# Cross-attention and FP4 feed-forward block: the circulant attention step moved from shifted copies to a real Fourier basis

## The chip, the cores and the metric

The kernel runs on one core of a Trainium2 chip. The metric is the device time of one execution in microseconds (us); lower is better. Engine names are those of the profile: PE (matrix products), PEld (its weight loads), DVE (vector engine), ACT (activation engine), POOL and SP (here SP issues nearly all transfers, POOL the adding ones).

## The reference, cut to what matters

x and ctx are 64 x 128 x 256 floats; `_layernorm` is the plain one.

```python
q = layernorm(x) @ Wq + bq;  k = v = ctx @ Wq + bq        # 16 channels
corr = real(ifft(fft(q) * conj(fft(k)))).mean(axis=(0, 1))   # 128 lags, over batch and channel
W_topk, I_topk = top_k(corr, 12);  W_topk = softmax(W_topk)
R3 = sum(w * roll(v, -shift) for w, shift in zip(W_topk, I_topk))
x = x + broadcast_over_16_heads(R3) @ Wout + bout
# feed-forward; fp4() quantises blocks of 16 to FP4 and back
u = fp4(layernorm(x))
h = silu(u @ fp4(w_gate).T) * (u @ fp4(w_up).T)
x = x + fp4(h) @ fp4(w_down).T
```

(In the source `K_TOP = int(2 * log(512))`, which is 12, and the FFT runs over the 128 positions.)

## The kernel before, in words

Tokens lie as 16 groups of rows (`q` = 0..15) of four tiles; a tile is 128 tokens x 256. There are 64 tiles, numbered `t`. Four output tables `O[0..3]` of the attention (128 x 257, the last column a row mean) serve all tiles: group `q` uses `O[q % 4]`.

**Opening.** SP loads x transposed (`xt`, 16 loads), then ctx (`ct`, 8 loads `c0`..`c7` of 1 MB), then `Wo`, `Bo`. PE projects x (L921) and ctx (`pk`, L1053); DVE and ACT normalise into `qT` (L863 to L892); 16 products `pg<-qT,kT` (L1076) add up the 128 x 128 matrix whose circulant sums are the correlation. In the gaps DVE quantises the three weight matrices; SP transposes them (L720).

**Bridge**, from the last `pg` to the first feed-forward product. `pg` is copied twice side by side into `Wcor` (L1091). `skew` (L336) runs seven predicated copies that shift row p by p places, bit by bit; a product with ones (L1365) then gives the 128 lags on every partition. Top 12 by MAX8 and MATCH_REPLACE8 (L1387 to L1406), exponentials on ACT (L1399), the weights into `M` (L1410), and `skew` again, so that `M` is the circulant matrix. PE multiplies it with `Wo` (L1441), `Wp` is scaled by 1/sum (L1446, L1448), and `Vn` (the transposed values, L1372 and L1378) times `Wp` plus `Bo` gives `O` (L1454, L1459, copies L1466).

**x stage** (`x_parts`), for a group: mean `neg` (L459), centring, block maxima, scales, rounding on DVE and ACT, then a transposition into `xT`, on PE for the first two pairs of tiles and by an SP transfer (L642) for the rest. `O` is added to X on DVE (L445) for groups 0 to 2 and by an adding transfer on POOL (L481) from group 3 on.

**Feed-forward** (`group_ops`), for a tile: 18 products `gu` (L1166), SiLU on ACT (L1172), `h` and its block maxima on DVE (L1179, L1189, L1203), scaling on POOL (L1218; three tiles on DVE), rounding on ACT (L1246, L1262), two products with the scales on DVE (`hl`, L1271), a transposition by SP into one of eight homes `hT` (two lie in `Wdn`, two in `kT`; L1306), then 17 products `pd` with Wd (L1315, L1317; below "Wd products"), the sum into X (L1334) and the store (L1341). `gu` has two PSUM slots, which before the first tile serve the bridge as `hot` and `pa`: tile 0 takes over `hot`, tile 1 `pa`, and tile t needs that `h` of tile t-2 is done. `hl` has two buffers of two tiles.

**What sets the order.** Every operation is recorded with a cost and a due time (`op`, class `Order`); a planner picks, engine by engine, the one due first among those it expects to be ready, and the program is emitted in that order. Each engine then runs its queue in order. The due time of a tile's Wd products is

```python
dl=at(t) + SLOT * (LC + GROW * min(t, END) / 64.0 + nt - 1 - i + (LATE if t >= END else 0)),
```

with `SLOT` = 5425 ns, `LC` = 4.5 and `GROW` = 6, so they trail the tile's `gu` by some slots more towards the end. The x stage of group `q` is due `min(MARGIN, LEAD[0] + LEAD[1] * q)` slots ahead of its first tile.

Of the kernel before, what the change touches and what calls it, by code (L numbers as in the profile page):

```python
# [33 lines left out]
SUB = 2.0**-16  # L34
MAGIC_SUB = 1.5 * 2.0**32
# [224 lines left out]
def xattn_ffn(ctx: ExitStack, tc: tile.TileContext, x, xt, cx, wq, bq, wo, bo, wgu, wd, out):  # L260
# [13 lines left out]
    MT = res.tile([P, P], F32, name="MT")  # L274

# [25 lines left out]
    bits_i = const.tile([P, 7], I32, name="bits_i")  # L301
    bits = const.tile([P, 7], U16, name="bits")
# [7 lines left out]
    for k in range(7):  # L310
        V.tensor_single_scalar(bits_i[:, k : k + 1], pidx, 64 >> k, ALU.bitwise_and)
    V.tensor_copy(bits, bits_i)
# [15 lines left out]

    def skew(W, key, **kw):
        for k in range(7):  # L330
            s = 64 >> k
            n = P + s - 1
            op(
                "V",
                220,
                lambda k=k, s=s, n=n: V.copy_predicated(  # L336
                    W[:, 0:n], bits[:, k : k + 1].broadcast_to([P, n]), W[:, s : s + n]
                ),
                w=[key],
                **kw,  # L340
            )

# [4 lines left out]
    LC = 4.5  # L347
# [4 lines left out]
    TC = 46000.0  # L352
    TQ = 42000.0
# [13 lines left out]
    LEAD = (0.5, 0.5)  # L367
# [5 lines left out]
    LOADS = "wq bq wg0 wg1 x0 wg2 x1 x2 x3 wd x4 x5 x6 x7 x8 x9 x10 x11 x12 x13 x14 x15 c0 c1 c2 c3 c4 c5 c6 c7 wo bo"  # L373
# [50 lines left out]
    def x_parts(R, q, i0, nt, fast, due, alu, pe_x=False, root=False, both=None, off=0):  # L424
# [197 lines left out]
        if pe_x:  # L622
            for i in tiles:
                pt = Q["pd"].new()

                def f_t(i=i, pt=pt):
                    for b in range(4):
                        src = T["xhl"].t[:, i, b // 2, (b % 2) * P : (b % 2) * P + P]
                        PE.transpose(pt.t.bitcast(F16)[:, b * P : (b + 1) * P], src, ident_h)

                op("PE", 300, f_t, r=[(T["xhl"], 0), (T["xhl"], 1)], w=[pt])

                def f_x(i=i, pt=pt):
                    dst, src = T["xT"].t[:, i].rearrange("p k n -> p (k n)"), pt.t.bitcast(F16)[:, 0 : 4 * P]
                    V.tensor_copy(dst, src) if fast else A.copy(dst, src)

                op("V" if fast else "A", 420 if fast else 590, f_x, r=[pt], w=[(T["xT"], i)], dl=due - 300, port=False)
        else:
            op(
                "SP",  # L640
                450 * nt,
                lambda: SP.dma_start_transpose(  # L642
                    sub("xT").rearrange("p t k n -> p (t k) n"), sub("xhl").rearrange("p t e n -> p (t e n)")
                ),
                r=[(T["xhl"], 0), (T["xhl"], 1)],
                w=[(T["xT"], i) for i in tiles],
                lat=LT,
                dl=due - 2000,
            )
# [9 lines left out]
    Bo = res.tile([P, D + 1], F32, name="Bo")  # L659
    kT = res.tile([P, 16, P], F32, name="kT")  # L660
    W = res.tile([P, 2 * P], F32, name="Wcor")
# [66 lines left out]
    def d_scales(pool, ring, loaded):  # L728
        dgd = pool.tile([P, P], F32, name="dgd")
# [6 lines left out]
        op("V", 130, lambda: V.tensor_scalar(dgd, ident, s1, None, ALU.mult), r=["s1"], w=["dgd"])  # L736
        pm_d = ring.new()
        op("PE", 430, lambda: PE.matmul(pm_d.t[:, 0:P], ones, dgd, start=True, stop=True), r=["dgd"], w=[pm_d], dl=18000.0)
# [31 lines left out]
    with ExitStack() as ph1:  # L770
# [21 lines left out]
        r_ct = S.ring(rp, "ct", [P, 2, 4, 256], F32, 5)  # L792
# [11 lines left out]
            "bo": (400, ["Bo"], lambda: SP.dma_start(Bo[:, 0:D], bo.partition_broadcast(P))),  # L804
# [10 lines left out]
        for j in range(8):  # L815
            loads[f"c{j}"] = (2580, [(cts[j], 0), (cts[j], 1)], lambda j=j: SP.dma_start(cts[j].t, cx[j]))
            for b in range(2):
                loads[f"c{j}{'ab'[b]}"] = (
                    1456,
                    [(cts[j], b)],  # L820
                    lambda j=j, b=b: SP.dma_start(cts[j].t[:, :, :, b * P : (b + 1) * P], cx[j][:, :, :, b * P : (b + 1) * P]),
                )
# [32 lines left out]
        mrow = wp.tile([P, P], F32, name="mrow")  # L855
# [184 lines left out]
        op("SP", 2464, tr(WgH, lambda: HgN.rearrange("p h c n -> p (h c n)")), r=["HN", (cts[7], 0)], w=["WgH"], dl=TD - 2000, lat=LL, after=prev)  # L1040
        wgl = op("SP", 2464, tr(WgL, lambda: LgN.rearrange("p h c n -> p (h c n)")), r=["LN", (cts[7], 0)], w=["WgL"], dl=TD - 2000, lat=LL, after=prev)
        loaded = (load_x(0, dl=TD, after=(wgl,)),)
        d_scales(wp, r_q, loaded)
        load_x(1, dl=TD + 9000, after=loaded)
        for j, b0, b1 in [(j, 0, 2) for j in range(7)] + [(7, 0, 1), (7, 1, 2)]:
# [4 lines left out]
            def f_k(ct=ct, pk=pk, c0=b0 * P, n=n):  # L1050
                for kt in range(2):
                    for g in range(4):
                        PE.matmul(  # L1053
                            pk.t[32 * g : 32 * g + 32, 0:n],
                            Wq[:, kt],
                            ct.t[:, kt, g, c0 : c0 + n],
                            start=(kt == 0),
                            stop=(kt == 1),
                            tile_position=(0, 32 * g),
                            skip_group_check=True,  # L1060
                        )
# [12 lines left out]
            def f_g(bs=range(2 * j + b0, 2 * j + b1)):  # L1074
# [13 lines left out]
        op(  # L1088
            "V",
            331,  # L1090
            lambda: V.tensor_copy(  # L1091
                W.rearrange("p (a s) -> p a s", a=2), pg.unsqueeze(1).broadcast_to([P, 2, P])
            ),
            r=["pg"],
            w=["W"],
        )
# [258 lines left out]
    M = cs.tile([P, 2 * P], F32, name="M")  # L1355
    Wp = cs.tile([P, 2, D + 1], F32, name="Wp")
    skew(W, "W")
# [7 lines left out]
    sums = op("PE", 220, lambda: PE.matmul(hot.t[:, 512 : 512 + P], ones, W[:, 0:P], start=True, stop=True), r=["W"], w=[pc])  # L1365
    for j in range(8):
        after = () if j < 2 else (sums,)
        pv = Q["pd"].new()

        def f_v(j=j, pv=pv):  # L1370
            for b in range(2):
                PE.transpose(pv.t[:, b * P : (b + 1) * P], kT[:, 2 * j + b], ident)  # L1372

        op("PE", 220, f_v, r=[("kT", 2 * j), ("kT", 2 * j + 1)], w=[pv], after=after)
        op(
            "A",
            270,
            lambda j=j, pv=pv: A.copy(  # L1378
                Vn[:, :, 2 * j : 2 * j + 2, :].rearrange("p g b c -> p b g c"),
                pv.t[:, 0:256].rearrange("p (b g c) -> p b g c", b=2, c=32)[:, :, :, 0:16],  # L1380
            ),
            r=[pv],
            w=["Vn"],
        )

    C = lambda: hot.t[:, 512 : 512 + P]
# [16 lines left out]
    op("A", 1300, lambda: A.activation(warm, c_half, AF.Sqrt), w=["tbl"], dl=TO)  # L1403
# [5 lines left out]
        335,  # L1409
        lambda: V.scalar_tensor_tensor(  # L1410
            M.rearrange("p (a s) -> p a s", a=2),
            C3.unsqueeze(1).broadcast_to([P, 2, P]),
            NEG,
            E.unsqueeze(1).broadcast_to([P, 2, P]),
# [5 lines left out]
        w=["M", "es"],  # L1420
    )
    skew(M, "M")
    op("V", 69, lambda: V.tensor_scalar(es, es, 0.5, None, ALU.mult), w=["es"])
    op("V", 75, lambda: V.reciprocal(es, es), w=["es"])

    jw = cs.tile([P, D], BF16, name="jw")
    for dst, key in ((Wo[:, 0], "Wo"), (Wo[:, 1], "Wo"), (Bo, "Bo")):
        op(
            "A",
            400,  # L1430
            lambda dst=dst: A.activation(
                jw, dst[:, 0:D], AF.Copy, scale=1.0 / D, accum_out=dst[:, D : D + 1]
            ),
            w=[key, "jw"],
        )
    for k in range(2):
        pr = Q["pd"].new()
        op(
            "PE",
            430,  # L1440
            lambda k=k, pr=pr: PE.matmul(pr.t[:, 0 : D + 1], M[:, 0:P], Wo[:, k], start=True, stop=True),  # L1441
            r=["M", "Wo"],
            w=[pr],
        )
        if k == 0:
            f = lambda pr=pr: A.activation(Wp[:, 0], pr.t[:, 0 : D + 1], AF.Copy, scale=es)  # L1446
        else:
            f = lambda pr=pr: V.tensor_scalar(Wp[:, 1], pr.t[:, 0 : D + 1], es, None, ALU.mult)  # L1448
        op("AV"[k], 390, f, r=[pr, "es"], w=[("Wp", k)])
    pb = Q["pd"].new()  # L1450
    for g in range(4):
        po, pn = ((pa, g), pa.t[:, 512 * g : 512 * g + D + 1]) if g < 3 else ((pb, 0), pb.t[:, 0 : D + 1])
        Vg = Vn[:, g].rearrange("p b (r e) -> p e (b r)", e=2)
        op("PE", 430, lambda pn=pn: PE.matmul(pn, ones[0:1], Bo[0:1], start=True, stop=False), r=["Bo"], w=[po], after=(sums,))  # L1454
        for e in range(2):
            op(
                "PE",
                430,
                lambda e=e, pn=pn, Vg=Vg: PE.matmul(pn, Vg[:, e], Wp[:, e], start=False, stop=(e == 1)),  # L1459
                r=["Vn", ("Wp", e)],  # L1460
# [5 lines left out]
            lambda g=g, pn=pn: A.copy(O[g], pn),  # L1466
            r=[po],
# [4 lines left out]
    for t in h_tiles:  # L1472
        op(
            "A",
            350,
            lambda t=t: A.activation(
                t[:, :, NF : NF + 2 * NB], ones[:, 0 : 2 * NB].unsqueeze(1).broadcast_to([P, 2, 2 * NB]), AF.Copy, scale=htiny
# [107 lines left out]
```

## Time and profile before

| | us |
|---|---|
| three runs | 439.36, 439.63, 443.25; median 439.63 |
| the profiled execution, own time | 438.03 |
| its span, first to last instruction | 435.9 |
| busy PE / DVE / ACT / POOL | 415.9 / 388.7 / 286.2 / 136.9 |
| mean granted clock of PE | 0.999 |
| last `pg` product to first `gu` product | 54.7 to 73.57 |
| first to last `gu` product (starts) | 73.57 to 409.0 |

Times below are microseconds from the start of the span. A line of the timeline gives start, duration, engine, line of the kernel, operation, output and inputs, shape and count; a bracket holds the idle time of the engine before it and who ended it. Matmuls overlap, so their start-to-start distance (0.43 us for two `gu` products of 512 columns) tells more than their duration. A line of waits gives the total, the count and the longest.

### The profile page before, as it was taken

To read this page: it belongs to the slowest core of one execution; us is meant where nothing else is said; L and a number is where in the kernel's file an instruction comes from. 1 tells how busy PE (TensorE), PEld (TensorE's weight loads), DVE (VectorE), ACT (ScalarE), POOL (GpSimd) and SP (SyncE) were. 2 spreads that over 40 slices of the span, in tenths; PEclk is the share of its full clock that TensorE was granted. 3 is DMA by queue.
4 is the path that set the end of the run, shared out by engine and by line. 5 is a ranking of instruction groups with operands and counts; after the bars stand their busy time and mean duration, and the time that the engine had idled before them with its cause. 6 is when DMAs were issued, how large, how long until landed. Compare 5 with 4: busy or idle time off the path is not lost.

```text
span 435.9 us, 7976 instructions
## 1 busy us (share of the span) xinstructions
PE 415.9 (95%) x2948; PEld 265.4 (61%) x2948; DVE 388.7 (89%) x832; ACT 286.2 (66%) x484; POOL 136.9 (31%) x121
## 2 busy tenths in 40 slices
PE   7999978889899999999999999999999999999996
PEld 6457655446555656566566666666665666566685
DVE  6999368999999999989999989999999999978872
ACT  2797547988596696467946794887579666464410
POOL 0000003044444264344444444454434222324100
PEclk9999999999999999999999999999999999999999
DMA  7999999253787588579767897687578615952362
GB/s 282 408 415 420 334 215 358 37 105 71 151 185 142 131 196 175 139 117 233 157 136 161 197 158 163 139 176 152 117 161 164 156 39 120 192 125 66 94 169 74
DMA packets 151495, 76.61 MB, mean 176 GB/s; under 512 B 134432, under 2 KB 141984, under 8 KB 150432
## 3 DMA queue, kind: packets, MB, share of 16 engines
q1 hardware_dynamic: 143968, 69.29, 59.5%
q0 software_dynamic: 7488, 6.82, 11.0%
q8 instruction: 23, 0.38, 0.4%
q14 instruction: 16, 0.13, 0.1%
HBM read 27.76 MB, written 8.39 MB: 83 GB/s over the span
## 4 chain that ended last, share of the span: by engine, by line
PE 61%; DVE 16%; DMA 9%; ACT 9%; issue 2%; SPq 1%; DVEq 0%; ACTq 0%
PE gu L1166 37%; PE pd L1315 14%; PE pd L1317 8%; DMA ct<-in_cx_dram 6%; DMA xt<-in_xt_dram 4%; DVE hs L1189 3%; DVE h L1179 2%; DVE hl L1271 2%; ACT junk L507 2%; ACT cc L497 2%; ACT g L1172 2%; DVE am L517 1%; ACT hk L1246 1%; ACT hc L1262 1%; DVE hr L1203 1%
## 5 line engine op out<-in xcount | busy, mean ns | idle before, releaser
L1166 PE MATMUL gu<-WgH,xT 128*128 128x512 f16 (+1 forms) x768 | 191.7, 361 | 5.5 <-ACT g L1172 1.5
L1166 PEld LDWEIGHTS <-xT 128*128 128x128 f16 x1152 | 112.4, 98 | 114.8 <-issue 4.5
L1218 POOL TENSOR_TENSOR h<-h,hr 128x704 f32<-128x704 f32 x61 | 92.8, 1521 | 199.0 <-DVE hr L1203 169.7
L1166 PE MATMUL gu<-WgL,xT 128*128 128x512 f16 (+1 forms) x384 | 107.4, 361 | 0.0
L1172 ACT ACTIVATE g<-gu,ug 128x704 f32<-128x704 f32 x64 | 53.6, 840 | 41.8 <-PE gu L1166 41.6
L1246 ACT ACTIVATE hk<-h,c_half 128x1408 int16<-128x1408 f32 (+1 forms) x34 | 47.4, 1394 | 37.3 <-POOL h L1218 34.5
L1189 DVE TENSOR_REDUCE hs<-h 128x44 f32<-128x792 f32 x64 | 66.7, 1042 | 2.1
L481 POOL DMA_DIRECT2D X<-O x52 | 45.7, 939 | 71.0 <-DMA X<-in_x_dram 71.0
L1179 DVE SCALAR_TENSOR_TENSOR h<-gu,uh,g 128x704 f32<-128x704 f32 x64 | 55.9, 874 | 5.0 <-ACT g L1172 3.2
L1262 ACT ACTIVATE hc<-hk,c_sub 128x1408 f16<-128x1408 int16 (+1 forms) x32 | 45.6, 1426 | 0.5
L1315 PE MATMUL pd<-WdH,hT 128*128 128x256 f16 x352 | 43.7, 273 | 1.2 <-DMA hT<-hl 1.2
L1315 PEld LDWEIGHTS <-hT 128*128 128x128 f16 x352 | 34.3, 98 | 9.5 <-DMA hT<-hl 1.6
L1334 DVE SCALAR_TENSOR_TENSOR X<-pd,ud,X 128x512 f32<-128x512 f32 (+1 forms) x34 | 24.3, 715 | 11.3 <-PE pd L1317 11.3
L497 ACT ACTIVATE cc<-X,neg 128x256 f32<-128x256 f32 x62 | 30.2, 497 | 3.6 <-DVE neg L459 2.9
L1271 DVE TENSOR_TENSOR hl<-hc,hsb 128x1408 f16<-128x1408 f16 (+1 forms) x34 | 28.7, 843 | 0.2
L1271 DVE TENSOR_TENSOR hl<-hc,hsl 128x1408 f16<-128x1408 f16 (+1 forms) x34 | 28.6, 841 | 0.0
L1203 DVE RECIPROCAL hr<-hs 128x44 f32<-128x44 f32 x64 | 26.8, 419 | 0.2
L507 ACT ACTIVATE junk<-cc 128x256 bf16<-128x256 f32 x64 | 25.9, 405 | 1.0 <-DVE cc L470 0.8
L1317 PE MATMUL pd<-WdL,hT 128*128 128x256 f16 x192 | 26.2, 273 | 0.0
L1232 ACT ACTIVATE hsb<-hs 128x176 bf16<-128x176 f32 (+1 forms) x34 | 11.4, 334 | 19.8 <-DVE hs L1189 19.8
L912 ACT ACTIVATE xsq<-xt,shift 128x1024 f32<-128x1024 f32 x16 | 18.1, 1148 | 9.5 <-DVE shift L908 7.0
L584 DVE TENSOR_TENSOR cc<-cc,rz 128x256 f32<-128x256 f32 x64 | 23.3, 418 | 0.1
(215 smaller groups left out, 532.9 us busy)
## 6 DMA issues: line engine op xcount, KB each, us to landing
xt<-in_xt_dram SPq DMA_DIRECT2D x16, 512.0 KB, 8.1
ct<-in_cx_dram SPq DMA_DIRECT2D x8, 1024.0 KB, 11.5
X<-in_x_dram SPq DMA_DIRECT2D x16, 512.0 KB, 4.5
out_dram<-X SPq DMA_DIRECT2D x30, 256.0 KB, 2.3
X<-O POOLq DMA_DIRECT2D x52, 128.0 KB, 2.8
Wg<-in_wgu_dram SPq DMA_DIRECT2D x2, 512.0 KB, 4.5
Wdn<-in_wd_dram SPq DMA_DIRECT2D x1, 704.0 KB, 9.6
hT<-hl SPq DMA_TRANSPOSE x32, 3.3
```

Source lines behind the costliest of these rows:

```text
L481: lambda i=i: G.dma_start(Xq.t[:, i0 + i], O[g][:, 0:D], accum_op=ALU.add),
L497: lambda i=i: A.activation(T["cc"].t[:, i], Xq.t[:, i0 + i], AF.Identity, bias=T["neg"].t[:, i : i + 1]),
L1166: PE.matmul(pg.t[:, c0:c1], src[:, b], w[:, k, c0:c1], start=(m == 0), stop=(m == 5))
L1172: lambda pg=pg, g=g: A.activation(g.t, pg.t[:, 0:NF], AF.Silu, scale=ug),
L1179: lambda pg=pg, g=g, i=i: V.scalar_tensor_tensor(B["h"].t[:, i, 0:NF], pg.t[:, NF:NG], uh, g.t, ALU.mult, ALU.mult),
L1189: lambda i=i: V.tensor_reduce(B["s"].t[:, i], B["h"].t[:, i].rearrange("p (jj b e) -> p b jj e", b=NB, e=2), AX.XY, ALU.max, apply_absolut ...
L1218: lambda i=i, zv=zv: (V if zv else G).tensor_tensor(per_block(B["h"].t[:, i, 0:NF], NB), per_block(B["h"].t[:, i, 0:NF], NB), spread(B["r" ...
L1246: lambda: A.activation(sub("k"), sub("h")[:, :, 0:NF], AF.Identity, bias=c_half, scale=24.0),
L1262: lambda: A.activation(flat("c"), flat("k"), AF.Identity, bias=c_sub, scale=SUB),
L1271: lambda e=e, part=part: V.tensor_tensor(B["hl"].t[:, 0:nt, e].rearrange("p t (jj n) -> p t jj n", jj=JJ), sub("c").rearrange("p t (jj n) ...
L1315: PE.matmul(pd, hT.t[:, b], WdH[:, :, b], start=(b == 0), stop=False)
L1317: PE.matmul(pd, hT.t[:, b], WdL[:, :, b], start=False, stop=(b == 5))
```

## The change

1. `skew` and its 14 predicated copies are gone. DVE makes a 128 x 128 table of sines and cosines during the opening (a saw-tooth of the index, folded, then a polynomial; `four`), PE transposes it (`fourT`).
2. Correlation: `pg` is copied once, one product with `fourT`, two products-with-sum on DVE give `uv`, two products bring the 128 lags onto every partition.
3. The weights `wm` are summed against the table (`wv`). Products of `Wo` and of `Vn` with the table (`J`, `B`, `Va`) do not need them and are issued ahead; `Wp` is put together from `J`, `B` and `wv`, and 1/sum is applied in the copies to `O`. The row means of `Wo` and `Bo` move from ACT to DVE.
4. ctx is laid out in half blocks, `c7` loaded as two; `Bo` is loaded into one partition, ahead of `c0`.
5. `LC` is 5.5 and `LEAD` (1.5, 0.5); the first `xT` copies are due 4 us earlier; the small constants in the `h` tiles (`least`) go from ACT to POOL.

```diff
-    LC = 4.5
+    LC = 5.5
-    LEAD = (0.5, 0.5)
+    LEAD = (1.5, 0.5)
-    LOADS = "... x15 c0 c1 c2 c3 c4 c5 c6 c7 wo bo"
+    LOADS = "... x15 bo c0 c1 c2 c3 c4 c5 c6 c7a c7b wo"
...
+        op("G", 300, lambda: G.iota(ang(), pattern=[[0, 2], [1, P]], base=0, channel_multiplier=0), w=[(scr, "ang")])
+        for k in range(2):
+            op("V", 170, lambda k=k: V.tensor_scalar(ang()[:, k], ang()[:, k], fr, 96.0 * k, ALU.mult, ALU.add), ...)
+        op("V", 300, lambda: V.tensor_single_scalar(ang(), ang(), 127, ALU.bitwise_and), w=[(scr, "ang")])
...
+        op("V", 330, lambda: V.scalar_tensor_tensor(four[:, 0:2], poly(), SIN[0], tri(), ALU.add, ALU.mult), ...)
...
-            W.rearrange("p (a s) -> p a s", a=2), pg.unsqueeze(1).broadcast_to([P, 2, P])
+        op("V", 220, lambda: V.tensor_copy(W, pg), r=["pg"], w=["W", "mrow"], dl=TC + 4000.0)
-    skew(W, "W")
-    sums = op("PE", 220, lambda: PE.matmul(hot.t[:, 512 : 512 + P], ones, W[:, 0:P], ...), r=["W"], w=[pc])
+    T_op = op("PE", 270, lambda: PE.matmul(C(), fourT[:, 0], W, start=True, stop=True), r=["W", "fourT"], w=[pc])
+    for k in range(2):
+            lambda k=k: V.scalar_tensor_tensor(jk, C(), wt, four[:, 2 + k], ALU.mult, ALU.mult, accum_out=uv[:, k : k + 1]),
+            PE.matmul(C(), uv[:, k : k + 1].broadcast_to([P, P]), four[:, k], start=(k == 0), stop=(k == 1))
...
-    skew(M, "M")
+    for k in (1, 0):
+            lambda k=k: V.scalar_tensor_tensor(jk, wm, (wt, nwt)[k], four[:, k], ALU.mult, ALU.mult, accum_out=wv[:, k : k + 1]),
+    op("V", 75, lambda: V.reciprocal(inv, es), r=["es"], w=["inv"])
+    op("V", 200, lambda: V.tensor_scalar(Wp[:, 0], JB, wv[:, 1:2], None, ALU.mult), ...)
+    t1_op = op("A", 450, lambda: A.activation(Wp[:, 1], spec["J", 1][1](), AF.Copy, scale=wv[:, 1:2]), ...)
+    op("A", 1300, lambda: A.activation(warm, c_half, AF.Sqrt), w=["tbl"], dl=TO, after=[*quick, t1_op])
+            lambda e=e, t=t: V.scalar_tensor_tensor(Wp[:, e], t(), wv[:, 0:1], Wp[:, e], ALU.mult, ALU.add),
+    for g in range(4):
+        bank = (2, 0, 1, 2)[g]
+            lambda pn=pn: PE.matmul(pn, es[0:1, 0:1].broadcast_to([1, P]), Bo, start=True, stop=False),
+                lambda e=e, pn=pn, Vg=Vg: PE.matmul(pn, Vg[:, e], Wp[:, e], start=False, stop=(e == 1)),
+            lambda g=g, pn=pn: A.activation(O[g], pn, AF.Copy, scale=inv),
```

As emitted, the tables `O[2]` and `O[3]` are finished after the first tile's `gu` products, on ACT behind a load of its function table, and in the same PSUM slot that tile 1's `gu` takes over.

## The prediction

> **What bounds the kernel now.** I read the chain that ended last first, then the engines by stretches, then the timeline of the bridge, then the waits of PE behind it.
>
> ```profile
> PE 61%; DVE 16%; DMA 9%; ACT 9%; issue 2%; SPq 1%; DVEq 0%; ACTq 0%
> ```
>
> ```profile
> 55.00:73.50 18.50, 14.77 (x86) 11.06 (x86) 14.15 (x52) 10.32 (x34) 1.01 (x2) 1.00 1.07 290
> 73.50:90.00 16.50, 13.98 (x76) 7.27 (x77) 16.33 (x39) 15.65 (x36) 3.54 (x4) 1.00 0.41 87
> 90.00:110.00 20.00, 20.00 (x117) 11.28 (x116) 19.60 (x47) 16.48 (x36) 10.52 (x9) 1.00 0.43 86
> 110.00:140.00 30.00, 26.32 (x166) 15.65 (x164) 29.48 (x67) 21.31 (x40) 12.77 (x12) 1.00 0.78 168
> 140.00:409.00 269.00, 267.69 (x1698) 165.90 (x1696) 252.51 (x492) 180.88 (x286) 108.17 (x89) 1.00 0.69 148
> ```
>
> Columns: stretch, length, busy time of PE, PEld, DVE, ACT, POOL, granted clock, DMA share, GB/s. From 140 to 409 PE is full and only its own work counts. From 73.5 to 140 DVE is full and PE stands still for 2.5 and 3.7 us. Before that neither is full: a chain through all engines sets the pace.
>
> ```profile
> 53.12 1.60 PE L1076 MATMUL pg<-qT,kT 128*128 128x128 f32 x12
> 54.77 0.42 DVE L1091 COPY Wcor<-pg 128x256 f32<-128x256 f32 x1 [7.38 <-PE pg L1076]
> 55.23 2.49 DVE L336 COPY_PREDICATED Wcor<-bits,Wcor 128x191 f32<-128x191 uint16 x7
> 61.34 1.70 DVE L336 COPY_PREDICATED M<-bits,M 128x143 f32<-128x143 uint16 x5
> 63.15 1.11 PE L1441 MATMUL pd<-Wo,M 128*128 128x257 f32 x4 [0.80 <-issue]
> 66.42 0.23 DVE L459 TENSOR_SCALAR neg<-MT,O 128x2 f32<-128x2 f32 x1 [1.64 <-ACT O L1466]
> 73.57 0.60 PE L1166 MATMUL gu<-WgH,xT 128*128 128x512 f16 x2 [0.56 <-DVE xT L635]
> 77.19 1.28 ACT L1495 ACT_TABLE_LOAD   x1
> ```
>
> The bridge takes 11.65 us from the copy at 54.77 to `neg` at 66.42, some 5 of them in two skews; another 7.15 lead to the first product at 73.57.
>
> ```profile
> PE gu L1166 <- DVE h L1179: 1.3, 1, 1.3
> PE pd L1315 <- DMA hT<-hl: 1.2, 1, 1.2
> PE pd L1315 <- DMA Wdn<-hl: 1.1, 1, 1.1
> PE gu L1166 <- ACT xT L635: 1.0, 1, 1.0
> PE gu L1166 <- DMA xT<-xhl: 0.8, 1, 0.8
> ```
>
> These are PE's waits between 66 and 141: twice for transposed `hl` (Wd products issued before their input), three times for h or xT.
>
> **Part 1, up to the last pg.** DVE gains the table. Six operations with two inputs of 128x256 at 0.35 start to start (L584: two in 0.76), four with one input at 0.25 (L592 takes 0.33 at twice the width), six of half width at 0.15 to 0.25 and a small reduction: 2.1 + 1.0 + 1.1 + 0.45, about 4.7 us; bounds 4 and 6. The cover is the 7.38 us that DVE idles ahead of L1091. As emitted, ten of these stand ahead of the chain rstd, qT, but the third LgN (0.94), a Wdn product (0.88) and the small scales (1.2) move behind it, so that chain stays within 0.3 us. PE's order changes: all four fan products (L873) now run first, ending near 45.3 (before 45.66), and after them come four `pk` (0.97 each), two halves (1.24), 16 `pg` (0.27 each) and three transpositions (0.47): 9.9, so the last `pg` ends at 55.2 instead of 54.72. That is +0.5; bounds -0.3 (PE fills its waits as before) and +4.7 (the whole table ahead of qT).
>
> The halved c7 buys nothing here: PE reaches its first half at 51.8, and the whole block landed at 51.3. The layout reads 4 KB runs instead of 8 KB. xt, which has 4 KB runs, moved 406 to 411 GB/s, ct 416 to 426, so 8.4 MB of ct take up to 0.6 us more; PE comes to the second half at 52.9, 1.0 later than even that. The Trainium skill (DMA: Bandwidth & Descriptors, Bandwidth) advises transfers of at least 1 MiB for 75% of peak, which speaks against halves; xt's 512 KB loads at 408 GB/s do not bear it out. By that page's table (0.95 us for 64 KB, 6.15 for 1 MB) I estimate two halves at 0.6 us more than one whole: by it the second half would land at 52.5, and the sum would stay. The 1 KB of Bo ahead of c0 costs one issue (0.58 at L804) in SP's queue, whose eight ct issues are spread over 16.3 us anyway, waiting for buffers.
>
> **Part 2, the bridge.** Out go the skews (2.49 and, 60.55 to 63.04, another 2.49) and the Wo product with its copy on the path. In its place, from 55.2: copy 0.30 (L863 reads PSUM at this width in 0.29); table product to its reader 0.64 (57.72 to 58.36 for L1365); two sums at 0.35 (L1410: 0.42 at twice the width plus a 0.08 read); two products to MAX8 0.96; MAX8 to the last weighting 1.73, unchanged (58.36 to 60.09); weighting 0.37; `wv`, 1/sum, `wv` 0.86; `Wp` 0.35 and two additions at 0.45 (L1448: 0.48); the last product 0.70; 0.30 because it stands behind its partner in PE's queue; the copy to `O` 0.41. Sum 8.2 (the accumulating forms and the broadcast weights are not in the trace: bounds 7.2, all at the rows of half the width, and 9.8, all at the full width). So `neg` runs at 63.45, 2.97 earlier. The sums of Wo (L517 at this width: 0.69) hide in the 0.96; the products J, B and Va hide on PE behind the MAX8 part; without that cover they cost eight times 0.55.
>
> The Sqrt table load (1.28, next operation 1.29 after it starts) now stands on ACT right ahead of O[0]; it ends at 62.6 and O's product at 62.95, so it is covered by 0.35. The Trainium skill (ScalarE: Activation LUTs, What ACT_TABLE_LOAD costs) adds a 1.38 us drain to each switch; the trace shows none here, but by that rule `neg` would come 1.0 later. X0 landed at 61.3 and X1 at 68.0, against needs at 63.7 and 69.5: the loads hide, X1 by 1.5 us only.
>
> The 7.15 us of the x stage are the same instructions, so the first `gu` starts at 70.6, -3.0.
>
> **Part 3, where the lead goes.** Tile 1's slot holds O[2] and O[3]. ACT copies them only behind the Silu table load, which ended 12.3 us after `neg`: 75.7, then some 0.5 later for the X addition moved back, then two copies. Tile 1 starts at 77.2, as before. It costs little: tile 2 (81.95) needs xT, and tile 3 needs h of tile 1, which DVE finishes at 85.7. I walked the emitted order with start-to-start times of the same rows: h of tile 0 at 80.75, then hs 1.0, a rounding 0.4, two xhl 1.35. Tile 3 starts at 85.8 against 88.75.
>
> Then the due times act. The first Wd product follows 7.3 tiles of `gu` instead of 5.7, and the lag stays 0.7 to 1 tile longer. Tile 4 starts at 90.6 (92.3 before), tile 6 at 98.4. `xhl` of group 2 ends on DVE at 109.05; its transfers make tile 8 start at 113.2 against 116.44, with PE idle for 4.0, and with two Wd products (3.7) fewer done. They are made up without waits: tile 12 starts at 134.9 against 136.5, six Wd products done in both. **Lead 1.6 to 1.7 us.** From here PE is full. Before lost another 1.3 after this point (0.97 at 174 for a SiLU); I take half of that as saved. Sum: -1.7 - 0.65 = -2.35.
>
> POOL's three small constants wait for O[3] at 77.1 and take 0.4 to 1.5 each (L1218 has four times the size), so they end between 78.3 and 81.6; the first hs runs at 81.6. Behind them in POOL's queue stand four adding transfers for group 3 (0.9 to 2.2 each, 2.8 to land), which land by 93 at the latest; ACT takes that group up after 95. SP's queue keeps its order of weights and X; an xT transfer waits behind one hT transfer, which is in the 113.2.
>
> The profiled execution, 438.03, becomes 435.7; the median of the runs shown stands 1.6 above it, so 439.63 becomes **437.3**.
>
> **Rivals.**
> *The early lead stays and the waits go* (faster): 2.95 at tile 3 plus the Wd, xT and h waits behind it (1.2, 1.1, 0.8, 0.6, 0.97) give -7.5, 432.1. For it: these are waits for inputs a tile late, which a longer lag meets. Against it: DVE is busy 29.5 of 30 us there, and its work is not less.
> *The lead is lost* before tile 12 (pg 1 us later, X1 or the table load late): 439.6.
> *The homes of hT* (slower): eight homes, and the lag of Wd products reaches 13.0 tiles instead of 12.0. Tile 58's transposition ran at 405.52, its home was free at 399.4, tile 59's at 402.2. As emitted those two Wd products move 1.33 tiles of `gu` (4.8 us) later, which eats the margin. If from the point where the lag exceeds what `gu` to `hl` takes plus eight, half of the last 17 pairs wait one Wd product (1.86), DVE, which idles under 1% from 200 to 350, pays 14.9, less 4.7 of slack at the end (hl of tile 63 at 422.9, transposed at 427.65), less 2.35: +7.8, 447.5. For it: SP already waits nine times on pd. Against it: never over 1.3 us.
>
> **How the numbers follow.** Forecast 0.50, lead lost 0.13, faster rival 0.25, slower rival 0.12. The forecast's own range is -4.2 (parts 1 and 2 at their lower ends: 0.8 and 1.0 off) to +0.5 (PE loses after tile 8 the 3.0 that it lost there before: 113.2 + 3.7 - 116.4): 435.4 to 440.1. The upper end of part 1 alone, with all of the table ahead of qT, gives +1.9, 441.5. The 8 in 10 takes that in and reaches towards both rivals: 432.0 to 442.5. One per cent, 4.4 us, is about what a measurement of this kernel can tell from no change: faster 0.25, same 0.62, slower 0.13.
>
> **What would show it.** The MAX8 at 57.75 and `neg` near 63.45; the first `gu` near 70.6, the second tile near 77.2; PE idle some 4 us ahead of tile 8; tile 12 near 134.9; the last `gu` near 407. Wrong if pg ends after 56, if ACT's load is what O[0] waits for, or if SP's waits on pd grow past 2 us.

## The result, and the profile after

The changed kernel takes 441.25 us (median of 20 runs, 439.28 to 444.02), the kernel before 439.37 (20 runs, 437.8 to 443.25): ratio 1.0044, interval 1.0025 to 1.0063. It is 1.9 us slower where 2.35 us faster was forecast.

The chain that ended last, of the changed kernel, and its engines by the stretches of before (columns as there; the granted clock is the third number from the end):

```profile
PE 73%; DVE 10%; ACT 8%; DMA 6%; issue 2%; SPq 1%; POOL 0%; ACTq 0%; DVEq 0%; POOLq 0%
```

```profile
55.00:73.50 18.50, 15.32 (x64) 9.63 (x63) 11.91 (x45) 10.85 (x32) 0.22 (x1) 0.85 1.07 278
73.50:90.00 16.50, 14.95 (x74) 8.15 (x73) 13.82 (x33) 12.81 (x31) 6.74 (x8) 0.86 0.37 78
90.00:110.00 20.00, 19.60 (x110) 10.57 (x109) 19.79 (x49) 15.67 (x29) 9.34 (x8) 1.00 0.51 89
110.00:140.00 30.00, 25.51 (x154) 15.36 (x153) 27.83 (x61) 24.07 (x49) 11.68 (x10) 0.89 0.72 142
140.00:409.00 269.00, 266.87 (x1685) 164.58 (x1683) 252.23 (x495) 179.88 (x283) 109.59 (x90) 1.00 0.79 149
```

The new thing is the clock: 1.00 in all these rows before, now 0.85, 0.86 and 0.89 in three. Finer windows show that it is 1.00 or 0.50 and changes on a grid of 3.41 us, which lies elsewhere in each execution:

```profile
64.43:67.85 3.42, 2.40 (x9) 1.51 (x10) 2.52 (x6) 1.78 (x8) 0.00 (x0) 1.00 0.89 238
67.85:71.26 3.41, 2.84 (x8) 1.47 (x7) 3.02 (x13) 2.75 (x11) 0.00 (x0) 0.50 1.02 404
71.26:74.67 3.41, 3.41 (x17) 2.44 (x17) 1.82 (x6) 2.28 (x9) 1.39 (x2) 0.50 1.02 417
74.67:78.09 3.42, 3.42 (x10) 1.22 (x9) 3.35 (x10) 2.59 (x9) 2.00 (x3) 0.50 0.36 79
112.22:115.63 3.41, 1.33 (x8) 0.56 (x6) 3.38 (x8) 1.38 (x4) 1.01 (x1) 1.00 0.86 165
115.63:119.05 3.42, 1.02 (x3) 0.43 (x4) 3.39 (x8) 2.85 (x2) 2.97 (x4) 0.50 1.09 194
119.05:122.46 3.41, 3.41 (x10) 1.21 (x8) 3.41 (x16) 1.73 (x6) 0.69 (x1) 0.50 0.70 127
```

Five stretches at half clock, behind two places where PE had too little to do: the bridge, and the pause ahead of tile 8. This profiled execution is the longest of the 20. An execution's stretches follow from its mean clock: (1 - clock) x span / 0.5 / 3.41, rounded. Median spans by their number, with how many executions in brackets:

| kernel | 0 | 1 | 2 | 3 | 4 and more |
|---|---|---|---|---|---|
| before (27, beside e1 to e4) | 435.9 (7) | | 437.4 (18) | 439.1 (1) | 440.9 (1) |
| changed | | 437.6 (2) | 439.3 (13) | 440.5 (2) | 441.5, 442.2 (3) |
| e1_fill | | 438.0 (5) | 439.2 (7) | | |
| e5_fill_both | 436.8 (5) | 437.3 (5) | 440.0 (2) | | |
| e6_fill_t8 | 436.1 (4) | 437.8 (8) | | | |
| e9_fill_grow5 | 435.5 (7) | 436.7 (5) | | | |
| e10_t8_grow5 | 435.0 (3) | 435.9 (1) | 437.8, 438.1 (2) | 438.7 (5) | 440.4 (1) |
| e12_onerow | | 437.1 (4) | 438.4 (8) | | |
| e13_bias_rows | | 437.7 (7) | 438.8 (4) | | 440.2 (1) |
| e14_best | 434.9 (10) | 434.6 (1) | 436.5 (1) | | |

The bridge and the pause, by the timeline of the changed kernel (start, length, engine, line; in brackets the idle time before and what ended it):

```profile
56.99 0.30 DVE L1464 MAX8 ma<-gu 128x8 f32<-128x128 f32 x1
61.41 0.49 DVE L1515 SCALAR_TENSOR_TENSOR Wp<-gu,wv,Wp 128x257 f32<-128x257 f32 x1 [0.91 <-ACT Wp L1508]
64.50 0.23 DVE L454 TENSOR_SCALAR neg<-MT,O 128x2 f32<-128x2 f32 x1 [2.22 <-ACT O L1541]
66.42 0.37 ACT L1461 COPY Va<-gu 128x256 f32<-128x256 f32 x1 [0.79 <-PE gu L1526]
66.69 0.42 ACT L502 ACTIVATE junk<-cc 128x256 bf16<-128x256 f32 x1
75.08 1.06 PE L1190 MATMUL gu<-WgH,xT 128*128 128x512 f16 x2
118.03 1.04 PE L1190 MATMUL gu<-WgH,xT 128*128 128x512 f16 x2 [4.49 <-DVE h L1203]
```

MAX8 and `neg` come earlier than before (58.36, 66.42), the first `gu` later (73.57): its two matmuls take 1.06 where 0.60 is usual. PE stands still for 4.49 ahead of tile 8. The bracket names the `h` that ended at 118.01; the transfer of tile 8's `xT` had landed only 0.02 earlier, at 117.99, and in e1 below the same pause ends with that transfer.

### The profile page after: what moved, and what is told of

The parts are those of the page before. It is cut to its first block, busy times and chain, and to the rows that moved or that the text cites. A ratio compares the mean times of both kernels' runs of the same rounds, so it can differ in the third digit from the quotient of the medians.

```text
span 442.2 us, 7970 instructions
## 1 busy us (share of the span) xinstructions
PE 422.5 (96%) x2934; PEld 268.2 (61%) x2934; DVE 390.9 (88%) x847; ACT 286.6 (65%) x477; POOL 140.1 (32%) x125
## 4 chain that ended last, share of the span: by engine, by line
PE 73%; DVE 10%; ACT 8%; DMA 6%; issue 2%; SPq 1%; POOL 0%; ACTq 0%; DVEq 0%; POOLq 0%
PE gu L1190 42%; PE pd L1339 15%; PE pd L1341 8%; DMA xt<-in_xt_dram 4%; DVE hs L1213 2%; DVE h L1203 2%; ACT g L1196 1%; DMA Wg<-in_wgu_dram 1%; DVE hl L1295 1%; PE pk L1047 1%; PE gu L1534 1%; PE pg L1070 1%; PE pm L867 1%; ACT hk L1270 1%; ACT hc L1286 1%
## 5 line engine op out<-in xcount | busy, mean ns | idle before, releaser
L1190 PE MATMUL gu<-WgH,xT 128*128 128x512 f16 (+1 forms) x768 | 194.8, 365 | 8.6 <-DVE h L1203 4.8
L1190 PE MATMUL gu<-WgL,xT 128*128 128x512 f16 (+1 forms) x384 | 108.8, 365 | 0.0
L593 ACT ACTIVATE k<-cc,c_half 128x1024 int16<-128x1024 f32 (+1 forms) x16 | 17.9, 1118 | 8.6 <-DVE cc L579 8.6
```

What stands on the lines that cost most here:

```text
L1190: PE.matmul(pg.t[:, c0:c1], src[:, b], w[:, k, c0:c1], start=(m == 0), stop=(m == 5))
```

## Experiments

**Fill in the bridge, with and without.** The kernel has identity products (L719, L724 before) that its emitter puts into PE's idle time as planned. In the bridge the kernel before has 16 of them, the changed one 4, since the planner books each new product at 530 ns and sees no idle time. e1_fill brings them to 16 (12 more, not the six that its expectation names); e2_nofill takes all but one of them out of the kernel before.

```
- for _ in range(int((at - self.free["PE"] - SPARE) / cost)):
+ for _ in range(o.extra + max(0, int((at - self.free["PE"] - SPARE) / cost))):
...  # e1: extra = 2 at the Va product of g 2, and at bias and Wp·Va for g > 0
     heat_buf(hot, TW)
+    S.fill.pop()   # e2, in the kernel before
```

> Theory A (clock): between the last pg and the first gu the changed kernel issues 4 fill products (identity by identity, L719) where the kernel before had 16, because its planner counts the new products at 530 ns each and sees no idle time; PE then streams for too small a share of one 3.41 us stretch and the granted clock falls to 0.5 for one or more whole stretches, each of which costs 1.7 us. Six fill products more, in the places where PE waits for ACT's copies, should hold the clock through the bridge: mean clock 0.996 or more in most executions, the time 1.5 to 3 us below the changed kernel's 441.25, at 438 to 439.7, ratio to before 0.997 to 1.001. Theory B (order): the clock only follows from PE's waits, and the time is lost to the order on ACT and PE (O[0] behind Va copies, tile 1 behind O[2] and O[3]); then the fill gains nothing and the ratio stays at 1.003 to 1.006.

> The kernel before without the 16 fill products of the bridge (they write nothing that is read). Theory A: PE streams for under half of at least one stretch of 3.41 us, the clock falls to 0.5 for 2 to 4 stretches, mean clock 0.985 to 0.992, and the time rises by 2 to 5 us, ratio 1.005 to 1.011. Theory B: the bridge is set by ACT and DVE, fill is idle work, ratio 0.999 to 1.001.

e1: 440.68, 1.0033 (1.0018 to 1.0047). e2: 441.17, 1.0049 (1.0031 to 1.0068), with three stretches or more in every execution. In the kernel before the fill is not idle work: without it the time rises. e1's ratio lies in Theory B's range, not in Theory A's: its trace shows the bridge at full clock, as Theory A said, but it gained only 0.6, with the stretches behind tile 8's pause still there:

```profile
65.30:68.71 3.41, 3.27 (x18) 2.55 (x17) 2.33 (x8) 2.36 (x10) 0.00 (x0) 1.00 0.89 347
109.54:112.96 3.42, 0.12 (x1) 0.00 (x0) 3.38 (x9) 1.53 (x2) 2.23 (x2) 1.00 1.10 209
112.96:116.37 3.41, 2.30 (x6) 0.89 (x7) 3.38 (x13) 3.19 (x5) 2.44 (x3) 0.50 1.09 203
116.37:119.78 3.41, 3.41 (x11) 1.36 (x9) 3.34 (x11) 1.08 (x4) 0.00 (x0) 0.50 0.39 65
```

**The due times.** e3_old_due sets LC 4.5 and LEAD (0.5, 0.5) in the changed kernel, e4_new_due the new values in the kernel before, e7_fill_lc LC 4.5 in e1_fill.

> The changed kernel with the due times of before (LC 4.5, LEAD 0.5), so only the Fourier part is left and the early xT copies. Theory A: the stretch at 112 to 116 us, where PE stood still ahead of tile 8, keeps more Wd products and the clock stays full there; only the bridge's stretches at half clock are left: mean clock 0.992 to 0.996 and 438.5 to 440, ratio 0.998 to 1.002. Theory B: the later due times saved waits, as forecast; without them 1 us more than the changed kernel, ratio 1.005 to 1.008.

> The kernel before with the later due times alone (LC 5.5, LEAD 1.5). Forecast's reading: fewer waits for hT, 0.5 to 1 us saved, ratio 0.997 to 0.999. Theory A: Wd products that filled PE's waits between 100 and 120 us are put off, PE stands still longer there, and one or two stretches at half clock appear ahead of tile 8: mean clock 0.992 to 0.996, ratio 1.003 to 1.008. If due times do not matter at all: 0.999 to 1.001.

> The fill of e1_fill, and the Wd products' due time back at LC 4.5 (LEAD stays at 1.5). Theory A: real work takes the place of the pause: four Wd products instead of two are done when tile 8 starts, as before, so the stretches there stay full as before: mean clock 0.996 or more; but a Wd product waits for hT once or twice (1.2 us each before): 437.5 to 439.5, ratio 0.997 to 1.001. Theory B (the later due times are what the gain hangs on, as e3_old_due's 1.0147 suggests): slower than e1_fill by 1 to 5 us, ratio 1.006 to 1.015.

e3: 445.57, 1.0147 (1.0123 to 1.017). e4: 441.39, 1.003 (1.0005 to 1.0054). e7: 444.26, 1.0119 (1.0094 to 1.0144). Theory A missed on e3 and e7; e3 is slower than either theory said, e7 within Theory B. In e7, with four Wd products done, PE waits 7.4 us ahead of tile 8, as DVE makes `xhl` for it at 116.36 instead of 107.75 (e1): earlier Wd work goes ahead of it on the engine that is full. The later due times are needed by the Fourier part. In the kernel before (e4, as Theory A said) they put off work that covered a wait: 2.8 us ahead of tile 8, with a stretch at half clock behind it; its trace has two more, in the bridge and behind the first `gu` products.

**Fill ahead of tile 8**, into its own buffer, overwritten by its products: e5 in e1_fill, e6 in the changed kernel.

```
+ for _ in range(6 if t == 8 and c0 == 0 else 0):
+     PE.matmul(pg.t[:, 0:P], ident, ident, start=True, stop=True)
```

> The fill of e1_fill in the bridge, and 6 identity products (12 instructions, 2.6 us) ahead of the products of tile 8, written into its own buffer and then overwritten; they can start once h of tile 6 is read, some 1.7 us after PE falls idle. Theory A (clock): e1_fill kept the clock full in the bridge and still lost 3.4 us to the two stretches at 112.96, behind the pause of 4.4 us ahead of tile 8. With the pause half filled, these stretches stay full: mean clock 0.998 or more in most executions, span 435.5 to 436.5, time 437.3 to 438.3, ratio 0.996 to 0.999. Theory B (order): the pause is there because xT is late, the time after it is set by DVE, and fill gains under 0.5 us: ratio 1.002 to 1.004 as in e1_fill.

> The changed kernel with the 6 identity products ahead of tile 8 alone, no fill added in the bridge. Theory A: the stretches behind tile 8's pause go (3.4 us, two stretches), those of the bridge stay (1 to 3 stretches, 0.75 to 1.7 us each): mean clock 0.989 to 0.997, 438 to 440, ratio 0.998 to 1.002. Theory B: as the changed kernel, 1.004.

e5: 438.98, 1.0006 (0.9978 to 1.0034). e6: 439.32, 0.9999 (0.9975 to 1.0024). e6 is within Theory A; e5 lies between the two theories, as only 5 of its 12 executions have no stretch at half clock. Some 2 us come back with work that computes nothing: the slowdown against the kernel before goes with the clock. In executions with no stretch at half clock e5 and e6 stand at 436.8 and 436.1, the kernel before, run beside them, at 435.8: the forecast gain is not there at full clock either.

**ACT's queue in the bridge.** e8_va_dve is e5 with three Va copies (L1461) on DVE.

> As e5_fill_both, and the copies of Va for the groups 1 to 3 are on DVE instead of ACT. In e1_fill ACT read the squares for the first x tile 2.18 us after neg, where the kernel before took 0.78: two Va copies stood ahead of them in ACT's queue, each waiting for PE. If that is where the bridge's lead of some 2 us at neg shrank to 0.9 us at the first gu, the first gu comes 0.8 to 1.4 us earlier than in e5_fill_both (near 71.5 instead of 72.7), and tile 1 near 77.5; at the end 0 to 1 us of it is left: ratio 0.994 to 0.998. If ACT's queue does not matter there: as e5_fill_both within 0.3 us.

e8: 440.7, 1.005 (1.0029 to 1.0071). The first `gu` came at 71.83 (e5 73.18), as expected; tile 1 at 79.40 and tile 8 at 116.21 (e5 79.14, 114.63). The time missed its range (0.994 to 0.998). A lead at the first `gu` does not reach tile 8: DVE, with no wait between 98 and 118, makes `xhl` for it at 110.50, where e5 has 108.25.

**The lag at the end.** e9 is e5 with 11 products ahead of tile 8 and GROW 5.0 for 6.0, e10 the same without the bridge's fill; e11 is the kernel before.

> As e5_fill_both, with 11 identity products (2.4 us) ahead of tile 8 instead of 6, which took only 1.65 us of the pause, and with GROW 5.0 instead of 6.0: the due times of Wd products then reach 12 tiles of lag at the end, as before, instead of 13. If the clock is what is left ahead of tile 8, the two stretches seen there in e5_fill_both go, and nearly every execution has 0 or 1 stretch at half clock. If the lag is what made PE wait twice for a SiLU near 345 and 366 us (0.87 and 0.86 us; the kernel before has one such wait, 0.97 at 174), one or both go: span 435.2 to 436.3, time 437.0 to 438.2, ratio 0.995 to 0.999. If neither matters: as e5_fill_both, 1.000.

> As e9_fill_grow5 without the fill added in the bridge: the bridge's stretch at half clock stays in two executions of three (0.7 to 1.7 us). Clock theory: 0 to 1.5 us above e9_fill_grow5, ratio 0.996 to 1.001. If the six fill products in the bridge delay the chain more than the clock costs: 0.3 to 0.7 us below e9_fill_grow5.

> The kernel before, unchanged: where its own stretches at half clock lie, which 18 of 27 of its executions have (two stretches, 1.5 us). The share of PE's streaming is lowest at the start of the span, at 69.5 to 73 and at 80 to 90 us of the trace of before; two stretches that cost only 0.75 us each can lie where PE is not the bound, at one of these. Clock 0.991 and span near 437.4 expected, or 0.999 and 435.9 in one case of three.

e9: 437.94, 0.9979 (0.9956 to 1.0001). e10: 440.08, 1.0013 (0.9977 to 1.0049). The two SiLU waits near 345 and 366 went (one of 1.24 came at 258), and the span without half clock fell from 436.8 to 435.5 (e10 against e6: from 436.1 to 435.0). Both changed the fill ahead of tile 8 and GROW at once, so that GROW did it is argued from those waits, not shown. e10 lies above its range (2.1 over e9 where 0 to 1.5 was expected): at full clock the bridge's fill costs 0.5, but without it 8 of 12 executions have two stretches or more, with it none. e11 fell on an execution at full clock (span 436.2), so where the kernel before has its two stretches stays open.

**What counts as activity.** I summed, for each stretch of the grid, the start-to-start times that PE's products take back to back (0.215 for 512 columns of f16 or 257 of f32). Here is the stretch ahead of the bridge's half clock, in groups of one form:

```profile
L1457 PE MATMUL gu<-Vn,fourT 128*128 128x256 f32 x3 | 1.3, 485 | 0.6 <-ACT O L1541 0.6
L1534 PE MATMUL gu<-Wp,Va 128*128 128x257 f32 x4 | 1.1, 409 | 0.5 <-ACT Va L1461 0.5
L1526 PE MATMUL gu<-Bo,es 1*128 1x257 f32 x2 | 0.7, 426 | 0.5 <-ACT Va L1461 0.5
```

Eight of them and the first 0.03 us of the ninth, which starts at the edge, make 1.73 of 3.41 us, 0.51; without the two one-row bias products 1.30, 0.38. Over all 16 traces from 50 to 425 us, 20 stretches at full clock were followed by one at half. By time their shares reach 0.73, and stretches at 0.39 stayed full; with one-row products left out, all 20 are at 0.383 or less, and no full one is below 0.375. The one at 0.73 is in e4, whose bridge has the products of the kernel before; PE is busy in it for 3.33 of 3.42 us, and the clock still falls:

```profile
57.83:61.25 3.42, 3.33 (x18) 2.26 (x18) 2.52 (x14) 1.05 (x4) 0.00 (x0) 1.00 0.88 182
61.25:64.66 3.41, 3.24 (x12) 2.42 (x10) 1.81 (x7) 2.41 (x6) 0.00 (x0) 0.50 1.19 253
```

In the two traces of the kernel before, the stretch there (from 59.28 and 59.12) comes to 0.38 and stayed full: its bridge stands at this edge, and is the likely place of its own two stretches, though no trace of it holds one. The way back follows the same count. Of 31 stretches at half clock, the 11 that were followed by another stream for up to 0.74 of their time, the 20 that were not for 0.75 or more; as a product takes twice as long there (two `gu` products 0.85 start to start in e1 from 115.75, 0.43 at full clock), that is the work of 0.37 to 0.38 at full clock. All this was found in the traces, so e12 and e13 test the part on rows: e12 is e9 with a one-row fill, e13 the changed kernel with the bias in 128 rows.

```
- PE.matmul(pg.t[:, 0:P], ident, ident, ...)          # e12
+ PE.matmul(pg.t[:, 0:P], ident[0:1, :], ident[0:1, :], ...)
- Bo = res.tile([1, D + 1], F32, name="Bo")           # e13
+ Bo = res.tile([P, D + 1], F32, name="Bo"); V.memset(Bo, 0.0)
- PE.matmul(pn, es[0:1, 0:1].broadcast_to([1, P]), Bo, ...)
+ PE.matmul(pn, es.broadcast_to([P, P]), Bo, ...)
```

> As e9_fill_grow5, but the 11 products ahead of tile 8 read one row of the identity instead of 128, so they take the same time on PE and work one row of the array. In 13 traces the stretches of 3.41 us that let the clock fall were streamed for up to 0.40 of their time, those that did not for more, with five exceptions at 0.51 to 0.73, all of which hold one-row products (the bias); counted at nothing, they all come to 0.38 or less. Theory rows (a product counts by the rows that it works): ahead of tile 8 the clock falls as if there were no fill, two stretches in nearly every execution, none at 0, span 438 to 440, ratio 1.001 to 1.004. Theory time (only PE's busy time counts): as e9_fill_grow5, 0 stretches in half of the executions, 437.9, ratio 0.998.

> The changed kernel with the bias row in a tile of 128 rows, 127 of them zero, so that the four bias products of the bridge work 128 rows in the same time; nothing else. Theory rows: the bridge's stretches (0.38 counted by rows, 0.51 by time, at 64.4) come to 0.5 and stay full in most executions; those ahead of tile 8 stay: 1 to 2 stretches instead of 1 to 5, 439.5 to 440.8, ratio 1.001 to 1.0035. Theory time: as the changed kernel, 441.25, ratio 1.0044.

e12: 440.06, 1.0005 (0.9981 to 1.0029); no execution without half clock, where e9 had 7 of 12. e13: 439.71, 1.0009 (0.9985 to 1.0032). Three windows of e9, then three of e12, then two of e13:

```profile
109.18:112.59 3.41, 1.51 (x13) 1.12 (x11) 3.38 (x7) 1.12 (x2) 1.81 (x2) 1.00 1.10 209
112.59:116.00 3.41, 3.41 (x18) 3.07 (x17) 3.38 (x12) 3.19 (x4) 2.86 (x3) 0.50 1.11 192
116.00:119.42 3.42, 3.42 (x22) 2.02 (x21) 3.35 (x12) 1.99 (x6) 0.00 (x0) 1.00 0.41 81
```

```profile
109.03:112.44 3.41, 1.51 (x12) 1.02 (x11) 3.38 (x7) 0.89 (x2) 1.59 (x2) 1.00 1.04 197
112.44:115.85 3.41, 3.41 (x18) 3.27 (x16) 3.38 (x13) 3.23 (x3) 2.96 (x3) 0.50 1.09 192
115.85:119.27 3.42, 3.42 (x9) 1.19 (x9) 3.39 (x13) 1.31 (x4) 0.12 (x1) 0.50 0.50 96
```

```profile
62.36:65.77 3.41, 2.38 (x9) 1.17 (x8) 1.74 (x5) 1.35 (x4) 0.00 (x0) 1.00 1.05 204
65.77:69.18 3.41, 2.38 (x11) 1.76 (x11) 2.33 (x9) 3.04 (x11) 0.00 (x0) 1.00 1.03 410
```

In the second stretch PE is busy for all 3.41 us in both, for the most part with the fill; behind 128-row products the clock comes back, behind one-row products not. In e13 PE is busy for 2.38 us, as for 2.40 in the changed kernel at 64.43, two of nine products being the bias in each; there the clock stayed full. One such stretch proves little, since one of e6 (65.66, 0.38 without its one-row products) stayed full as well. The count does more: 7 of 12 executions of e13 have only one stretch, in its trace the one behind tile 8's pause (113.56); of the changed kernel 2 of 20. Both times lie just below the ranges of Theory rows (from 1.001), further from those of Theory time (0.998 and 1.0044).

**A version that beats both.** e14 has GROW 5.0, the bias in 128 rows, no fill added in the bridge, and the pause filled from its start: 8 identity products behind tile 7's into free columns of its buffer, then 11 into tile 8's.

```
+ for _ in range(8 if t == 7 and c1 == NG else 0):
+     PE.matmul(pg.t[:, NG : NG + P], ident, ident, start=True, stop=True)
```

> The changed kernel with GROW 5.0, the bias in 128 rows, no fill added in the bridge, and the pause ahead of tile 8 filled from its start: 8 identity products behind tile 7's into 128 columns of its buffer that it leaves free, 11 into tile 8's buffer. If the clock is all that stands between the change and its gain: 0 stretches in most executions, span 434.6 to 435.6, time 436.4 to 437.5, ratio 0.994 to 0.9975. If the products behind tile 7 make ACT's SiLU wait for them (1.7 us): 0.5 to 1.7 us above that.

e14: 436.7 us against 439.4, ratio 0.994 (0.9918 to 0.9962), within the range for a clock that stays full. At full clock it stands at 434.9, the kernel before at 435.9: 1.0 of the 2.7 us. The rest comes from the two or more stretches that 22 of the 29 executions of the kernel before have here; fill for those places in the kernel before was not tried. The pause is still there, and filled:

```profile
109.30 1.95 PE L1195 MATMUL gu<-ident 128*128 128x128 f32 x16
111.36 2.69 PE L1191 MATMUL gu<-ident 128*128 128x128 f32 x22
113.92 0.60 PE L1193 MATMUL gu<-WgH,xT 128*128 128x512 f16 x2
```

## Why the prediction was wrong

The forecast (-2.35) and the result (+1.9) lie 4.2 us apart. At full clock the change is worth +0.3 (e6) to +1.0 us (e5). So 0.9 to 1.6 of the 4.2 are the clock, for which the sum had no term (net of what the kernel before loses to its own stretches), and some 2.6 to 3.4 are a lead that was smaller than forecast and did not last. e5 and e6 hold filler products besides the change, so this split is an estimate.

- **The step that failed**, and made it slower, is "tile 8 start at 113.2 ..., with PE idle for 4.0". The pause came (4.49; 4.41 in e1, tile 8 at 114.07), but I priced it as lost time alone. It also halves the clock behind it, for one stretch (e13) or two (e1); filling it in e6 brought 1.9 us back. No term of the sum had a clock, since every row that I read said 1.00, and I never asked what the 18 matmuls of L724 at 68.81 in the kernel before were for. The 1.6 us by which the runs stood above the profiled execution, which I carried over as a constant, were a sign of it: they match two stretches of the kernel before (spans 435.9 and 437.4). The range (to 442.5) held the time, the sign was wrong. The Trainium skill (TensorE: Matmul & The Clock Gate, HAM oscillation — how this bites in real kernels) warns of PE idle gaps over some 3.4 us; the 4.49 agrees. The bridge goes further: its longest gap there was 0.57.
- **Part 1**: no loss; the last `pg` ended at 54.19, not 55.2, and MAX8 came at 56.99 against 57.75 forecast. (L592, read as 0.33, takes 0.43; the table stayed hidden all the same.)
- **Part 2**: the cover of J and B failed. `E` and the J and B products took turns, and the additions to `Wp` waited 0.91 for ACT: `neg` at 64.50, not 63.45. Then "the same instructions" was wrong: the stage has the same ones, but in ACT's queue two Va copies now stand ahead of the squares, which start 2.19 behind `neg` (before 0.78). With the clock full there, the first `gu` ran at 72.68 (e1) and 72.21 (e13), 0.9 and 1.4 ahead of before, where 3.0 was forecast.
- **Part 3**: with the clock full (e14) tile 8 starts at 113.92 and tile 12 at 135.61, 0.8 ahead of before; forecast 113.2 and 134.9. That these came so near does not bear out part 2, as e8's lead at the first `gu` did not reach tile 8. So of the sum's first term, a lead of 1.7, half was there. The second, a saving of 0.65 behind tile 12, was of the wrong sign: PE waits 2.1 us for ACT's SiLU behind 141 instead of 1.0. At GROW 5.0 (e9, e10) 1.2 were left. Here are these waits, before and after:

```profile
PE gu L1166 <- ACT g L1172: 1.0, 1, 1.0
PE gu L1190 <- ACT g L1196: 2.1, 3, 0.9
```

- **The rivals**: SP's waits on pd grew from 5.4 us (9 times) to those below (total, times, longest), the longest under the 2 us that I named. Behind 141 PE waits for the SiLU alone, never for `hT`, so the homes of hT did not decide; whether the longer lag is behind the SiLU waits stays open. DVE idles 4.3% from 200 to 350 (143.58 of 150.00 us busy), not under 1%, so it could have taken up part of what that rival charges it. The terms of the faster one add up to -7.6, not -7.5.

```profile
SPq L1330 <- PE pd L1341: 14.3, 17, 1.8
```

## What to carry to other kernels

A pause of the matrix engine is priced twice: its length, and up to half of each 3.41 us stretch that runs at half clock behind it (1.7 us each in the changed kernel, 0.75 in the kernel before). One profile with a mean clock of 0.999 does not show that a kernel is free of such stretches: the kernel before had two in 18 of 27 executions. Before a forecast, add up what PE streams in the sparsest 3.41 us of each stage, leaving one-row products out, and see whether the change thins it; if filler products stand there, a change to the plan moves them too. And a lead is only worth what the next full engine lets through: follow it to the first stage where another engine is at 98%.

## What the runs showed of the hardware

I had not expected that the clock falls without any long gap, when products working 128 rows stream for under about 0.38 of a 3.41 us stretch, nor that products of one row count for nothing in it, to let it fall (0.51 by time at 64.43) or to bring it back (e12, 3.41 busy at half clock). Products of between 1 and 128 rows were not tried. The clock came back behind stretches at half clock that held at least the same work (0.75 of their time). The grid lies elsewhere in each execution, and the changed kernel has 1 to 5 such stretches, the kernel before 0 to 4, which goes with most of the spread between their runs: 1.7 us for each in the changed kernel (437.6 to 439.3), half of that in the kernel before (435.9 to 437.4 for two).
